# Shared expert of a mixture-of-experts layer: gate and up products from eight half-size products to seven, side by side

## The chip, the cores and the metric

The kernel runs on one core of a Trainium2 chip. The profile names the core's engines PE (TensorE, matrix products; PEld is its loading of stationary operands), DVE (VectorE), ACT (ScalarE), POOL (GpSimd) and SP (SyncE, which here only issues transfers). The metric is device time in microseconds (us) of one execution; the program is run several times and the median counts. One more execution is taken by the hardware profiler, and everything that is read engine by engine comes from that one.

## The reference

A two-layer network over a graph of 625 nodes with 1024 features each: graph attention, linear attention, a quantised feed-forward block, a graph convolution, a second linear attention, softmax attention, and last a mixture of experts. All data are 32-bit floats. The change lies in the last part:

```python
logits = xf @ Wr.T + expert_bias
rw = jax.nn.softmax(logits, axis=-1)
topw, topi = jax.lax.top_k(rw, TOP_K)
topw = jax.nn.softmax(topw, axis=-1)
combine = jnp.sum(jax.nn.one_hot(topi, NUM_EXPERTS, dtype=xf.dtype) * topw[..., None], axis=1)
shared = _swiglu(xf, sW1, sW2, sW3)
```

with `_swiglu(x, w1, w2, w3) = (silu(x @ w1.T) * (x @ w3.T)) @ w2.T`. `xf` is 625 x 1024; `sW1` (gate), `sW3` (up) and `sW2` (down) are 1024 x 1024. Each node also goes to two of eight routed experts of the same form.

## The kernel before

The node features are kept transposed, as `tT`: 128 partitions x 8 chunks of the 1024 features x 626 columns (625 nodes and one zero). Columns 0 to 312 are called `head` in the changed code, 313 to 625 `tail`. A product accumulates over feature chunks: the stationary operand is a 128 x 128 block of a weight, the moving one 313 columns of `tT`. One such matmul in the source shows as two instructions in the trace, so 256 matmuls show as x512. All are recorded at L137, in the helper `group`.

**Shared expert.** `hidden(m)`, for m = 0 to 7, makes 128 hidden features for all nodes: the gate product and the up product over all eight chunks, first for one half of the columns and then for the other, 64 instructions in all. Then ACT takes the sigmoid (L1783) and DVE multiplies twice (L1784, L1785) into `hT`. Gate and up weights come in `Half` tiles, two loads of 1 MB for 512 output columns of one matrix.

**Order.** This part stands in a `manual_schedule`: each engine's order is the order of the source. The `Stream` object `do(prep, pe, after)` writes the PE work of a step, and writes the steps that empty the accumulators (`after`) at the next call, ahead of that call's PE work. DVE, ACT and PE take their own instructions strictly in the order so written. Accumulators of the `ps2` kind are three. Weight tiles come from the pool `w`, with six buffers of 1 MB; a load waits on SP's queue until its buffer's last reader has finished, and later loads wait behind it. The pool `mid` has four larger buffers, `big` two. After the manual part the compiler's own scheduler orders the instructions.

**Routing steps.** Between the `hidden` calls stand the steps that decide who goes to which expert: `logits` (PE, 32 instructions), `turn_logits` (PE) and a chain of small DVE steps from `lg` (L1839) to `both` (L1880), here called chain one; `ranks` (PE, `prt`) and a second chain from `rank` (L1893) to `in_blk` (L1934) and `meta` (L1946), chain two; `tokens` (PE, `psl`), which gives `slots` (L1953). POOL's gathers of expert inputs (L1965) wait for `slots`, and SP reads the expert number for each weight load from `meta`. The order was: `hidden` 0, logits, `hidden` 1, turned logits, chain one, `hidden` 2, ranks, chain two, `hidden` 3, tokens, `hidden` 4 to 7.

**Experts.** `block(b)` gathers 128 rows (`xg`), transposes them on PE (`pxg`, L1972), DVE scales them into `xgT` (L1442), and then come the products with W1 and W3 (`pu`) and W2 (`pyb`), whose weights are 12 MB a block. W1 and W3 use the pool `w`, W2 the pool `mid`. The shared down projection's weights `sw2` are loaded between the blocks' weights, and `py` (last stage) uses them.

**The earlier graph layer.** One layer earlier (`Quarter`, `quarter`, `product`), the kernel already makes a block product of two halves by two halves from seven half-size products in place of eight. With blocks 11, 12, 21, 22 of the weights, DVE first makes combinations of weight tiles in place (`third`, `second`, `first`, `fourth`, all through `mix`, L1258) and of the columns (`S1` to `S4`), and adds up the seven results as they leave the accumulators (L1354). It is done twice, for two sets of columns.

Of the kernel before, what the change touches and what calls it, by code (L numbers as in the profile page):

```python
# [8 lines left out]
FP = mybir.dt.float32  # L9
# [4 lines left out]
AF = mybir.ActivationFunctionType  # L14
ALU = mybir.AluOpType
# [8 lines left out]
HN = 313  # L24
# [6 lines left out]
KC = D // 128  # L31
# [22 lines left out]
def attempt(ctx: ExitStack, tc: tile.TileContext, w: dict, out: bass.AP, shifted: bool):  # L54

    nc = tc.nc
# [10 lines left out]
    def ps2(name):  # L67
        return psums[-1][0].tile([128, 2, 512], FP, tag="ps2", name=name, bufs=3)
# [44 lines left out]
    class Half:  # L113


        def __init__(self, pool, src, c, tag="w", padded=None, now=True):
            v = src.rearrange("(k p) n -> p k n", p=128)
            self.parts = []

            def load():  # L120
                i = len(self.parts)
                t = pool.tile([128, 4, 512], FP, tag=tag, name="w", padded_shape=padded)
                self.parts.append(t)
                return nc.sync.dma_start(out=t, in_=v[:, 4 * i:4 * i + 4, c * 512:(c + 1) * 512])
# [9 lines left out]
    def group(dst, pairs):  # L134

        for i, (lhsT, rhs) in enumerate(pairs):
            made = nc.tensor.matmul(dst, lhsT=lhsT, rhs=rhs, start=(i == 0), stop=(i == len(pairs) - 1))  # L137
        latest["pe"] = made.ins.name

    latest = {}  # L140

# [13 lines left out]
    def halves(ap):  # L155
        return ap.rearrange("p (h n) -> p h n", h=2)
# [56 lines left out]
    wpool = graph.enter_context(tc.tile_pool(name="w", bufs=6))  # L213
# [3 lines left out]
    mix = mixed_up.enter_context(tc.tile_pool(name="mix", bufs=1))  # L217
# [145 lines left out]
    with ExitStack() as st0:  # L363
# [8 lines left out]
        with ExitStack() as edges:  # L372
            pool = edges.enter_context(tc.tile_pool(name="l0e", bufs=1))
# [21 lines left out]
            def load_edges():  # L395
                for dst, name in ((si, "src"), (di, "dst")):
# [16 lines left out]
                                      in_=none.unsqueeze(1).to_broadcast([128, 28, 440]))  # L413
# [4 lines left out]
            at = pool.tile([128, EN], I32, name="at")  # L418
# [24 lines left out]
            part = dict(done=0, held=0)  # L443
# [790 lines left out]
            rows_of(1, m)  # L1234
    meanT = []

    class Quarter:


        def __init__(self, i):  # L1240
            lo = 256 * i
            self.i = i
            self.tiles = {}
            self.source = {"12": ("W_self0", 512 + lo), "11": ("W_self0", lo),
                           "22": ("W_neigh0", 512 + lo), "21": ("W_neigh0", lo)}

        def room(self, name):
            self.tiles[name] = wpool.tile([128, KC, 256], FP, tag="w", name="wq" + name)

        def load(self, *names):  # L1250
            for name in names:
                self.room(name)
                src, lo = self.source[name]
                nc.sync.dma_start(out=self.tiles[name],
                                  in_=w[src].rearrange("(k p) n -> p k n", p=128)[:, :, lo:lo + 256])

        def mix(self, dst, a, b, op):
            nc.vector.tensor_tensor(self.tiles[dst], self.tiles[a], self.tiles[b], op=op)  # L1258

        def third(self):  # L1260
            self.mix("12", "22", "12", ALU.subtract)

        def second(self):
            self.mix("2", "12", "11", ALU.add)

        def first(self):
            self.mix("11", "22", "2", ALU.subtract)

        def fourth(self):
            self.mix("21", "21", "2", ALU.subtract)  # L1270

    quarters = [Quarter(0), Quarter(1)]
    quarters[0].room("2")
    quarters[0].load("12", "21", "11", "22")
    for k in range(KC):
# [55 lines left out]
    A12, A22 = ([meanT[k // 4][:, k % 4, h] for k in range(KC)] for h in (head, tail))  # L1331
    S1k, S2k, S3k, S4k = ([S[:, k, :] for k in range(KC)] for S in (S1, S2, S3, S4))

    def quarter(q):
        i = q.i
        kept = {}
        u = spool.tile([128, 2, HN], FP, tag="u", name="u", bufs=2)
        u3 = spool.tile([128, 2, HN], FP, tag="u", name="u3", bufs=2)

        def pairs(name, a, right):  # L1340
            wt = q.tiles[name]
            return [(wt[:, k, a * 128:(a + 1) * 128], right[k]) for k in range(KC)]

        def product(name, right, after):
            def pe():
                kept[0] = ps2("pw")
                for a in range(2):
                    wt = q.tiles[name]
                    group(kept[0][:, a, :HN], [(wt[:, k, a * 128:(a + 1) * 128], right[k]) for k in range(KC)])

            return lambda: do(None, pe, lambda: after(kept[0][:, :, :HN]))

        def add(dst, a, b):
            nc.vector.tensor_tensor(dst, a, b, op=ALU.add)  # L1354

        def done(c, h, a, b):
            dst = hT[c][:, 2 * i:2 * i + 2, h]
            add(dst, a, b)
            for a in range(2):
                m = 4 * c + 2 * i + a  # L1360
                nc.scalar.activation(dst[:, a, :], dst[:, a, :], AF.Relu, bias=b0_t[:, m:m + 1])

        def both(p):
            done(1, tail, p, u3)
            add(u, p, u)

# [10 lines left out]
    p1, p2, p6, p7, p4, p5, p3 = quarter(now)  # L1377
    four(sum1)
    four(sum2)
    p1()  # L1380
# [12 lines left out]
    then.third()  # L1393
    p3()
    then.room("2")
    p1, p2, p6, p7, p4, p5, p3 = quarter(then)
    p1()
    then.second()
    p2()
# [318 lines left out]

    (shifted_attention if shifted else attention)()
    wo = [Half(wpool, w["Wo"], c) for c in range(2)]  # L1720

    attn.close()
    pool = ctx.enter_context(tc.tile_pool(name="exp", bufs=1, reuse_waits="tile"))
# [37 lines left out]
        project(t)  # L1761
        turn_rows(tT, t - 1, 1)
    hT = bigT("hT")
    sw13 = [None, None]

    def hidden_halves(m):

        if m % 4 == 0:
            sw13[:] = [Half(wpool, w["sW1"], m // 4), Half(wpool, w["sW3"], m // 4)]
        w1, w3 = sw13  # L1770

        def piece(h):
            def pe():
                if h == 0:
                    hold["p13"] = [ps2("p1"), ps2("p3")]
                for p, wt in zip(hold["p13"], (w1, w3)):
                    group(p[:, h, :HN], [(wt(k, m % 4 * 128, 128), tT[:, k, h * HN:(h + 1) * HN])
                                         for k in range(KC)])

            def after():  # L1780
                p1_, p3_ = hold["p13"]
                sg = pool.tile([128, 2, HN], FP, tag="su", name="sg", bufs=2)
                nc.scalar.activation(sg, p1_[:, :, :HN], AF.Sigmoid)  # L1783
                nc.vector.tensor_tensor(sg, p1_[:, :, :HN], sg, op=ALU.mult)  # L1784
                nc.vector.tensor_tensor(halves(hT[:, m, :]), p3_[:, :, :HN], sg, op=ALU.mult)  # L1785

            do(None, pe, after if h else None)

        return piece

    def hidden(m):
        piece = hidden_halves(m)
        piece(0)
        piece(1)

    h0 = hidden_halves(0)
    h0(0)
    turn_rows(tT, NT - 1, 1)
    h0(1)
    eb_t = pool.tile([P, NE], FP, name="eb_t")  # L1800
    nc.gpsimd.dma_start(out=eb_t, in_=w["expert_bias"].to_broadcast([P, NE]))
    lg = pool.tile([P, NT, NE], FP, name="lg")
# [31 lines left out]
    nc.gpsimd.memset(place, 0)  # L1834

    do(None, logits, lambda: nc.vector.tensor_copy(halves(lgT), hold["plT"][:NE, :, :HN]))
    hidden(1)
    do(None, turn_logits)
    nc.vector.tensor_tensor(lg, hold["pl"][:P, 0:NT * NE].rearrange("p (t e) -> p t e", t=NT),  # L1839
                            eb_t.unsqueeze(1).to_broadcast([P, NT, NE]), op=ALU.add)  # L1840
# [38 lines left out]
    both = pool.tile([P, NT, NE], FP, name="both")  # L1879
    nc.vector.tensor_tensor(both, hots[0], hots[1], op=ALU.add)  # L1880
    flat = both.rearrange("p t e -> p (t e)")
    hidden(2)

    def ranks():
        hold["prt"] = ps1("prt")
# [58 lines left out]
    nc.vector.tensor_scalar(meta[:, NB + 1:NB + 2], within, -1.0, 512.0, op0=ALU.mult, op1=ALU.add)  # L1944
    nc.vector.tensor_scalar(meta[:, 0:NB], exp_f, float(NE - 1), None, op0=ALU.min)
    nc.vector.tensor_copy(meta[:, NB:NB + 1], ends[3][:, NE - 1:NE])  # L1946
    hidden(3)

    def tokens():
        hold["psl"] = ps1("psl")  # L1950
        group(hold["psl"][:, 0:NB], [(in_slot[:, i, :], in_blk[:, i, :]) for i in range(2 * NT)])

    do(None, tokens, lambda: nc.vector.tensor_scalar(slots, hold["psl"][:, 0:NB], float(N), None, op0=ALU.add))  # L1953
    for m in range(4, KC):
        hidden(m)
    do.flush()
    hand.close()

# [189 lines left out]
```

## Time and profile before

| | us |
|---|---|
| median of three runs | 2175.14 (2166.97 to 2180.34) |
| profiled execution, its own time | 2148.84 |
| its span, first to last instruction | 2147.1 |
| earlier graph layer's seven products, first to last matmul start | 777.4 to 895.3 |
| shared expert's stage, from its first matmul | 1395.4 |
| first expert's transposes (`pxg`) | 1542.4 |
| last stage (`py`) | from 2070.3 |

The profile gives each engine's busy time, and for groups of instructions the count, the busy time, the mean length of one, and the idle time of the engine just before them with what ended it. A matmul row shows the length of one instruction from start to a modelled end; neighbours overlap. Times are counted from the span's start.

### The profile page before, as it was taken

What the parts mean: (1) busy time and instruction counts of PE and PEld (TensorE: products, weight loads), DVE (VectorE), ACT (ScalarE), POOL (GpSimd) and SP (SyncE); (2) the same over time, 40 slices, a digit from 0 to 9 for tenths busy, and PEclk for the clock granted to TensorE, in tenths of its full rate; (3) what the DMA queues carried; (4) which work ended last, traced back from release to release, by engine and by line L of the source; (5) the groups of instructions that cost most, each with busy time, mean ns of one, the idle gap of its engine ahead of it and who ended that gap; (6) DMA issues with size and microseconds to landing.
All of it is one profiled execution on the core that took longest, in us unless ns stands there. A gap on an engine that the chain in (4) does not pass through costs nothing. (4 is left out here: it accounts for less than half of the span.)

```text
span 2147.1 us, 17319 instructions
## 1 busy us (share of the span) xinstructions
PE 2072.1 (97%) x6870; PEld 1184.0 (55%) x6870; DVE 754.5 (35%) x1250; ACT 197.6 (9%) x365; POOL 303.5 (14%) x321
## 2 busy tenths in 40 slices
PE   7999999399999999999999999999999999999998
PEld 6665574255446777644457776467644444444443
DVE  5786486576433772200121324222111111111012
ACT  2010110011211100000000111010000000000000
POOL 1777767200000000100000000100000000000011
PEclk9999999799999999999999999999999999999999
DMA  6632362440202102412121101202399889887832
GB/s 221 214 109 84 101 218 84 111 144 1 99 29 79 56 30 72 167 40 78 39 68 60 59 1 40 95 32 98 130 366 344 294 301 330 327 313 267 304 131 83
DMA packets 152022, 301.64 MB, mean 140 GB/s; under 512 B 12411, under 2 KB 33794, under 8 KB 151926
## 3 DMA queue, kind: packets, MB, share of 16 engines
q1 hardware_dynamic: 131356, 251.49, 33.2%
q0 software_dynamic: 15584, 38.66, 5.6%
q10 hardware_dynamic: 4986, 10.22, 1.5%
q8 instruction: 59, 0.97, 0.2%
q14 instruction: 37, 0.30, 0.0%
HBM read 277.49 MB, written 22.84 MB: 140 GB/s over the span
## 5 line engine op out<-in xcount | busy, mean ns | idle before, releaser
L137 PE MATMUL pu<-w,xgT 128*128 128x512 f32 x768 | 333.9, 593 | 1.9 <-DVE xgT L1442 1.9
L137 PEld LDWEIGHTS pu<-w,xgT 128*128 128x128 f32 x768 | 144.0, 190 | 174.8 <-issue 171.7
L137 PE MATMUL pyb<-w,hb 128*128 128x512 f32 x384 | 174.3, 599 | 2.4 <-ACT yb L105 2.1
L137 PE MATMUL pk<-w,xnT 128*125 128x512 f32 x320 | 143.5, 602 | 2.2 <-ACT xnT L1065 2.2
L137 PE MATMUL pv<-w,xnT 128*125 128x512 f32 x320 | 140.8, 593 | 0.9 <-DVE x L947 0.9
L137 PE MATMUL pq<-xnT,w 128*128 128x313 f32 x512 | 137.5, 427 | 0.8 <-DVE v L293 0.8
L137 PE MATMUL p<-tT,w 128*128 128x313 f32 x512 | 136.3, 428 | 0.4 <-DVE tT L1442 0.4
L1982 DVE TENSOR_TENSOR su<-pu,su 128x512 f32<-128x512 f32 x24 | 16.6, 691 | 314.6 <-ACT su L1981 314.6
L137 PEld LDWEIGHTS pyb<-w,hb 128*128 128x128 f32 x384 | 69.8, 189 | 90.9 <-issue 74.8
L137 PEld LDWEIGHTS pq<-xnT,w 128*128 128x128 f32 x512 | 96.9, 190 | 39.1 <-DVE v L293 1.6
L137 PEld LDWEIGHTS p<-tT,w 128*128 128x128 f32 x512 | 96.8, 190 | 37.9 <-issue 1.2
L766 PE MATMUL px<-w,oT 128*125 128x512 f32 x160 | 72.9, 615 | 32.0 <-DMA table<-es,at 26.7
L137 PEld LDWEIGHTS pk<-w,xnT 128*125 128x125 f32 x320 | 60.3, 191 | 75.8 <-issue 72.9
L137 PEld LDWEIGHTS pv<-w,xnT 128*125 128x125 f32 x320 | 59.4, 188 | 73.5 <-issue 71.2
L641 POOL DMA_INDIRECT table<-es,at x79 | 85.5, 1082 | 58.3 <-issue 28.4
L1965 POOL DMA_INDIRECT xg<-rows_d,slots x12 | 11.4, 948 | 524.7 <-PE pxg L1972 449.0
L621 POOL DMA_INDIRECT ga<-xl_d,si x79 | 79.2, 1003 | 30.1 <-issue 21.8
L621 POOL DMA_INDIRECT gb<-xr_d,di x79 | 78.6, 995 | 24.1 <-issue 20.7
L766 PEld LDWEIGHTS px<-w,oT 128*125 128x125 f32 x160 | 30.9, 196 | 71.6 <-issue 37.4
L137 PE MATMUL px<-w,hT 128*125 128x512 f32 x160 | 70.3, 592 | 0.0
L137 PE MATMUL px<-w,oT 128*125 128x512 f32 x160 | 70.3, 592 | 0.0
L137 PE MATMUL pX<-w,aT 128*125 128x512 f32 x160 | 69.3, 592 | 0.0
(376 smaller groups left out, 2443.0 us busy)
## 6 DMA issues: line engine op xcount, KB each, us to landing
w<-in_eW_dram SPq DMA_DIRECT2D x144, 1024.0 KB
w<-in_L_Wk_dram SPq DMA_DIRECT2D x8, 1024.0 KB
w<-in_L_Wv_dram SPq DMA_DIRECT2D x8, 1024.0 KB
w<-in_L_Wq_dram SPq DMA_DIRECT2D x8, 1024.0 KB
w<-in_L_Wo_dram SPq DMA_DIRECT2D x8, 1024.0 KB
w<-in_sW_dram SPq DMA_DIRECT2D x8, 1024.0 KB
table<-none SPq DMA_DIRECT2D x1, 6160.0 KB
y_d<-yb ACTq DMA_DIRECT2D x12, 512.0 KB
```

Of the source, the lines that this page charges most:

```text
L137: made = nc.tensor.matmul(dst, lhsT=lhsT, rhs=rhs, start=(i == 0), stop=(i == len(pairs) - 1))
L621: got = nc.gpsimd.indirect_dma_start(out=ab[g][side][0:p, j, :], out_offset=None, in_=src[:, :], in_offset=bass.IndirectOffsetOnAxis(ap=ix ...
L641: put = nc.gpsimd.indirect_dma_start(out=table[:, :], out_offset=bass.IndirectOffsetOnAxis(ap=at[0:p, lo + j:lo + j + 1], axis=0), in_=es[ ...
L766: made = nc.tensor.matmul(hold["px", t][:P, c, :], lhsT=oT[:, k, nodes(t)], rhs=wo[c](k), start=(k == 0), stop=(k == KC - 1 and keep is no ...
L1965: nc.gpsimd.indirect_dma_start(out=xg, out_offset=None, in_=rows_d[:, :], in_offset=bass.IndirectOffsetOnAxis(ap=slots[:, b:b + 1], axis=0))
L1982: nc.vector.tensor_tensor(su, pu[:, 0, :], su, op=ALU.mult)
```

## The change

The class `Quarter` moves to the kernel's beginning and takes the parts that its tiles are made of; for the graph layer it makes the same tiles as before. The shared expert uses it too. The blocks are the two halves of the features (`front`, chunks 0 to 3, and `back`, 4 to 7), of the output columns, and of the nodes. Each tile of 1 MB holds four chunks of the gate weight and, next to them, the same four of the up weight, for 256 output columns, so that one `mix` on DVE combines both. `eighth(i)` makes the seven products for one set of columns (i = 0, 1): each product is two halves, j = 0 for the gate and j = 1 for the up, with eight matmuls each. Results are kept in `uu` and added up as they leave the accumulators. When a gate block is complete ACT takes its sigmoid, and when the up block is complete DVE multiplies twice.

The routing steps keep their own order and now stand between single products of the first set: products one and two, logits, p6, turned logits and chain one, p7, ranks and chain two, p4, tokens, p5, p3, then the second set. `S12`, `S34` and the two `uu` take the four buffers of the pool `mid`.

```diff
-            self.source = {"12": ("W_self0", 512 + lo), "11": ("W_self0", lo),
-                           "22": ("W_neigh0", 512 + lo), "21": ("W_neigh0", lo)}
+            self.source = {name: [(src, k, lo + 512 * (name[1] == "2")) for src, k in parts[int(name[0]) - 1]]
+                           for name in ("11", "12", "21", "22")}
...
+                for src, k, lo in self.source[name]:
+                    n = k.stop - k.start
+                    nc.sync.dma_start(out=self.tiles[name][:, at:at + n, :],
+                                      in_=w[src].rearrange("(k p) n -> p k n", p=128)[:, k, lo:lo + 256])
+                    at += n
...
     wo = [Half(wpool, w["Wo"], c) for c in range(2)]
+    front, back = slice(0, 4), slice(4, KC)
+    quarters = [Quarter(256 * i, *([("sW1", k), ("sW3", k)] for k in (front, back))) for i in range(2)]
+    quarters[0].load("11", "21")
...
-    h0 = hidden_halves(0)
-    h0(0)
+    S12, S34 = (mid([128, 2, 4, HN], name) for name in ("S12", "S34"))
+    S1, S2, S3, S4 = (S[:, i] for S in (S12, S34) for i in range(2))
+
+    def eighth(i):
+        q = quarters[i]
+        uu = mid([128, 4, 2, HN], "uu")
+        kept = {}
+
+        def product(name, right, after):
+            def of(j):
+                def pe():
+                    kept[j] = ps2("ph13")
+                    for a in range(2):
+                        group(kept[j][:, a, :HN], [(q.tiles[name][:, 4 * j + k, a * 128:(a + 1) * 128], right[:, k, :])
+                                                   for k in range(4)])
+
+                do(None, pe, lambda: after(j, kept[j][:, :, :HN], uu[:, j], uu[:, 2 + j]))
...
+        def done(j, c, h, a, b):
+            dst = hT[:, 4 * c + 2 * i:4 * c + 2 * i + 2, h]
+            got = pool.tile([128, 2, HN], FP, tag="su", name="got", bufs=2)
+            if j == 0:
+                add(dst, a, b)
+                nc.scalar.activation(got, dst, AF.Sigmoid)
+                kept["gate"] = got
+            else:
+                add(got, a, b)
+                for part in (kept["gate"], got):
+                    nc.vector.tensor_tensor(dst, dst, part, op=ALU.mult)
+
+        def both(j, p, u, u3):
+            done(j, 1, tail, p, u3)
+            add(u, p, u)
+
+        return [product("11", tT[:, front, head], lambda j, p, u, u3: nc.scalar.activation(u, p, AF.Copy)),
+                product("21", tT[:, back, head], lambda j, p, u, u3: done(j, 0, head, p, u)),
+                product("2", S2, lambda j, p, u, u3: add(u, p, u)),
+                product("12", S3, lambda j, p, u, u3: add(u3, p, u)),
+                product("21", tT[:, back, tail], lambda j, p, u, u3: done(j, 0, tail, p, u3)),
+                product("11", S1, both),
+                product("22", S4, lambda j, p, u, u3: done(j, 1, head, p, u))]
+
+    now, then = quarters
+    now.load("12", "22")
+    now.room("2")
+    p1_, p2_, p6_, p7_, p4_, p5_, p3_ = eighth(0)
+    p1_()
     turn_rows(tT, NT - 1, 1)
-    h0(1)
+    add(S1, tT[:, front, tail], tT[:, back, tail])
+    nc.vector.tensor_tensor(S2, S1, tT[:, front, head], op=ALU.subtract)
+    now.third()
+    now.second()
+    then.load("12")
+    p2_()
+    now.first()
+    nc.vector.tensor_tensor(S3, tT[:, front, head], tT[:, front, tail], op=ALU.subtract)
...
-    hidden(1)
+    p6_()
+    now.fourth()
+    then.load("11")
...
-    hidden(2)
+    nc.vector.tensor_tensor(S4, tT[:, back, head], S2, op=ALU.subtract)
+    p7_()
+    then.load("22")
...
-    hidden(3)
+    p4_()
+    then.load("21")
...
-    for m in range(4, KC):
-        hidden(m)
+    p5_()
+    then.third()
+    p3_()
+    then.room("2")
+    p1_, p2_, p6_, p7_, p4_, p5_, p3_ = eighth(1)
+    p1_()
+    then.second()
+    p2_()
+    then.first()
+    p6_()
+    then.fourth()
+    p7_()
+    p4_()
+    p5_()
+    p3_()
     do.flush()
```

More of the change, by code (lines that the diff above doesn't have):

```diff
@@ L138, in group, with __init__, room, load @@
         latest["pe"] = made.ins.name
+    class Quarter:
+        def __init__(self, lo, *parts):
+            self.tiles = {}
+            self.source = {name: [(src, k, lo + 512 * (name[1] == "2")) for src, k in parts[int(name[0]) - 1]]
+                           for name in ("11", "12", "21", "22")}
+        def room(self, name):
+            self.tiles[name] = wpool.tile([128, KC, 256], FP, tag="w", name="wq" + name)
+        def load(self, *names):
+            for name in names:
+                self.room(name)
+                at = 0
+                for src, k, lo in self.source[name]:
[3 more added lines that the diff above has]
+                    at += n
+        def mix(self, dst, a, b, op):
+            nc.vector.tensor_tensor(self.tiles[dst], self.tiles[a], self.tiles[b], op=op)
+        def third(self):
+            self.mix("12", "22", "12", ALU.subtract)
+        def second(self):
+            self.mix("2", "12", "11", ALU.add)
+        def first(self):
+            self.mix("11", "22", "2", ALU.subtract)
+        def fourth(self):
+            self.mix("21", "21", "2", ALU.subtract)
+    def add(dst, a, b):
+        nc.vector.tensor_tensor(dst, a, b, op=ALU.add)
     latest = {}
@@ L1235, in attempt @@
     meanT = []
[L1237 to L1243, printed above, removed]
-            self.source = {"12": ("W_self0", 512 + lo), "11": ("W_self0", lo),
-                           "22": ("W_neigh0", 512 + lo), "21": ("W_neigh0", lo)}
[L1247 to L1272, printed above, removed]
+    every = slice(0, KC)
+    quarters = [Quarter(256 * i, [("W_self0", every)], [("W_neigh0", every)]) for i in range(2)]
     quarters[0].room("2")
@@ L1332, in attempt, with quarter @@
     S1k, S2k, S3k, S4k = ([S[:, k, :] for k in range(KC)] for S in (S1, S2, S3, S4))
-    def quarter(q):
-        i = q.i
+    def quarter(i):
+        q = quarters[i]
         kept = {}
@@ L1338, in quarter @@
         u3 = spool.tile([128, 2, HN], FP, tag="u", name="u3", bufs=2)
-        def pairs(name, a, right):
-            wt = q.tiles[name]
-            return [(wt[:, k, a * 128:(a + 1) * 128], right[k]) for k in range(KC)]
         def product(name, right, after):
@@ L1351, in product @@
             return lambda: do(None, pe, lambda: after(kept[0][:, :, :HN]))
-        def add(dst, a, b):
-            nc.vector.tensor_tensor(dst, a, b, op=ALU.add)
         def done(c, h, a, b):
@@ L1376, in attempt @@
     then.load("12")
-    p1, p2, p6, p7, p4, p5, p3 = quarter(now)
+    p1, p2, p6, p7, p4, p5, p3 = quarter(0)
     four(sum1)
@@ L1395, in attempt @@
     then.room("2")
-    p1, p2, p6, p7, p4, p5, p3 = quarter(then)
+    p1, p2, p6, p7, p4, p5, p3 = quarter(1)
     p1()
@@ L1763, in attempt @@
     hT = bigT("hT")
[L1764 to L1794, printed above, removed]
-    h0 = hidden_halves(0)
-    h0(0)
-    turn_rows(tT, NT - 1, 1)
-    h0(1)
+    S12, S34 = (mid([128, 2, 4, HN], name) for name in ("S12", "S34"))
+    S1, S2, S3, S4 = (S[:, i] for S in (S12, S34) for i in range(2))
+    def eighth(i):
+        q = quarters[i]
+        uu = mid([128, 4, 2, HN], "uu")
[8 more added lines that the diff above has]
+                do(None, pe, lambda: after(j, kept[j][:, :, :HN], uu[:, j], uu[:, 2 + j]))
+            def both():
+                of(0)
+                of(1)
+            return both
+        def done(j, c, h, a, b):
[19 more added lines that the diff above has]
+                product("22", S4, lambda j, p, u, u3: done(j, 1, head, p, u))]
```

## The prediction

> **What bounds the kernel now.** I read the page's first part, then the busy time by stretches, to see whether the shared expert's stage (1395.4 to 1542.1 us) and those around it leave TensorE idle.
>
> ```profile
> PE 2072.1 (97%) x6870; PEld 1184.0 (55%) x6870; DVE 754.5 (35%) x1250; ACT 197.6 (9%) x365; POOL 303.5 (14%) x321
> ```
> ```profile
> core 0: us, PE busy (x) PEld busy (x) DVE busy (x) ACT busy (x) POOL busy (x), PEclk, DMA share, GB/s
> 777.00:895.50 118.50, 118.50 (x452) 85.23 (x451) 42.38 (x35) 8.41 (x16) 7.67 (x13) 1.00 0.30 102
> ...
> 1395.40:1542.10 146.70, 146.26 (x575) 102.11 (x574) 28.49 (x83) 11.28 (x16) 6.32 (x11) 1.00 0.17 59
> 1542.10:2060.00 517.90, 514.23 (x1329) 233.59 (x1328) 65.16 (x96) 28.08 (x47) 9.39 (x10) 1.00 0.85 311
> ```
>
> In the changed stage PE idles 0.44 us of 146.7, at full clock, beside a DVE at 19% and DMA at 17%; the experts after it leave PE 3.7 us idle in 518. A microsecond of PE removed here comes off the end unless a new wait appears. The first stretch is the earlier graph layer, which is already made as seven products, with PE never idle. Next, the groups of the changed stage, then the rows of the earlier stage's tiles:
>
> ```profile
> L137 PE MATMUL p<-tT,w 128*128 128x313 f32 x512 | 136.3, 428 | 0.4 <-DVE tT L1442 0.4
> L137 PEld LDWEIGHTS p<-tT,w 128*128 128x128 f32 x512 | 96.8, 190 | 37.9 <-issue 1.2
> L137 PE MATMUL plgT<-tT,wr 128*8 128x313 f32 x32 | 8.6, 427 | 0.0
> ```
> ```profile
> L1354 DVE TENSOR_TENSOR hT<-pw,u x8: 809/809/810, 794.5 to 895.7; 128x626 f32<-128x626 f32 x8
> ...
> L1258 DVE TENSOR_TENSOR wq<-wq,wq x8: 2280/2282/2293, 766.7 to 854.3; 128x2048 f32<-128x2048 f32 x8
> ```
>
> A matmul is shown with 428 ns, but they overlap, so the pace counts. In the earlier stage 448 instructions of this shape run from 777.39 to 895.53, 0.2637 us each; in the changed stage 32 take 8.43 us start to start, 0.2634. Last, the timeline of the routing steps:
>
> ```profile
> 1440.33 0.19 DVE L1839 TENSOR_TENSOR lg<-plg,eb_t 125x40 f32<-125x40 f32 x1
> 1445.44 0.19 DVE L1880 TENSOR_TENSOR both<-hot,hot 125x40 f32<-125x40 f32 x1
> 1457.09 0.31 PE L137 MATMUL prt<-both,before 125*125 125x40 f32 x2
> 1458.02 0.19 DVE L1893 COPY rank<-prt 125x40 f32<-125x40 f32 x1
> 1464.73 0.34 DVE L1934 TENSOR_TENSOR in_blk<-in_blk,token 125x170 f16<-125x170 f16 x1
> 1474.60 0.41 PE L137 MATMUL psl<-in_blk,in_slot 125*128 125x17 f16 x10
> ```
>
> Chain one (lg to both) takes 5.3 us and PE asks for it 11.6 us later; chain two (rank to in_blk) takes 7.05, and PE asks 9.5 us later. That cover is what the change halves.
>
> **Removed.** Eight half-size products become seven: 512 instructions become 448 (the built order holds 224 source matmuls, two instructions each). 64 x 0.2634 = 16.9 us. A rule speaks against taking it whole: the Trainium skill, "Perfetto Trace Analysis", Identifying the Most-Contended Engine, says that the busy share of matmuls is a bad measure of how near TensorE is to its limit, and that weight loads should be read instead. Those are 102 of 146.7 us here, 70%; taken as the limit, 64 loads of 0.190 give 12.2 us. I take 16.9: the pace is a distance between starts, which no modelled end enters, and the earlier stage keeps it with the same weights and widths.
>
> Also gone: the 0.44 us in which PE waited for the last transposed rows of tT, since product two reads only the first 313 columns; and on DVE 16 instructions of 0.81 us.
>
> **Added on DVE, all beside PE if PE never waits for it.** Eight mixes of weight tiles at 2.28 = 18.2 us. S1 to S4, 1252 wide; the earlier stage does two such in 2.82, so 1.41 each, 5.6 us. Per pass (half the columns) 22 adds and multiplies 626 wide, 44 x 0.81 = 35.6 us (the multiplies lie between SBUF tiles; 0.71 by the S row, 0.81 by the hT row; I take 0.81). DVE goes from 28.5 to about 75 us in some 130: not a bound by volume. But it works in order, so each PE wait has to be followed through the first pass. With PE at 8.43 us a product:
> - PE: product one 1395.4, transposes 1.0, product two 1404.9 to 1413.4, logits to 1421.9, p6 to 1430.3, turned logits 0.7, p7 1431.0 to 1439.4, ranks 0.9, p4 1440.3 to 1448.8, token matmuls.
> - p6 needs S2 and two mixes. tT ends at 1405.8, two sums 1408.6, two mixes 1413.2; asked at 1421.9. Spare 8.7. The mixes need tiles 12 and 22, issued as their buffers come free: the four weight issues of before, which waited for the same buffers, ran from 1384.5 over 10.7 us, and the DMA they caused had ended by 1402. Spare again.
> - Ranks need chain one. Ahead of it DVE has product two's drains, two mixes, S3 and p6's drains; the last p6 drain can begin at 1430.4 and ends at 1431.2, then 5.3 us: 1436.5, asked at 1439.4. Spare 2.9. The exponential's table load is 1.3 us on ACT, which before preceded the chain, and does so again.
> - S4 and p7's drains follow (to 1440.3), then chain two from about 1440.6: in_blk at 1447.6, asked at 1448.8. Spare 1.2, the smallest.
> - Queued behind chain two is p4's first drain, 1449.3; its accumulator, one of three, is wanted by p5's second half at 1453.4. Spare 4.
>
> So I cost all DVE work at nothing, with PE as its cover. Without that cover, a late chain costs its lateness one for one. Between 0 and 3 us for the smallest spare, I take 0.
>
> **Moved loads.** The 8 MB come in 512 KB pieces with rows of 1 KB instead of 2. Between 803 and 807 a 1 MB load of such rows landed in 4.2 us at up to 378 GB/s; the longer rows reached 414. Bounds for 1 MB: 4.2, or 8.4 if the two pieces don't overlap. The latest one, tile 22 of the second pass, is issued once p7 is read (1439.5) and mixed at about 1455: hidden by either. On SP these waits stand ahead of the experts' first weights. In the built order W1 and W3 of the first block's first half are issued at about 1466, 1491, 1500 and 1508, against 1472 to about 1538 before. Then come four shared down-projection pieces (2 MB, some 5.5 us at 380 GB/s), done by 1514; the next expert weight waits for a buffer until 1516.6. W2 now waits for the sums' and u's last reader (about 1526), but stands behind W3, which waits for PE until about 1534. Cost 0; bounds minus 10 (second rival) and plus 5.5, were those pieces to hold a weight up by their whole length. POOL's gathers wait for slots, which come 24 us earlier.
>
> **Entry to the experts.** After the last product DVE has two drains before the first xgT step, and one between the two, where before it had one in all. First expert matmul after the transposes' start: 1.66 us before, now 2.4. Plus 0.7; bounds 0 and 1.5.
>
> **Sum.** -16.9 - 0.4 + 0.7 = -16.6 us. The profiled execution took 2148.84 us (span 2147.1): 2132.2, -0.77%. The median of the runs, 2175.14, is 1.2% above it; scaled alike, 2158.3, so 2158.
>
> **Rivals.** The bound is 1%, 21.7 us, about what a measurement of this kernel can tell from no change (its three runs span 13 us).
> - *Part of the gain is lost.* Weight loads set the pace (-12.2), or small waits at ranks, tokens and half-product drains take 5 to 10 us. For: the spare of 1.2, a DVE that is dense in the first pass. Against: the earlier stage has the same drains, and no PE wait. Time: 2163 to 2170.
> - *More than counted.* The experts have DMA at 0.85 in the profile; if ordinary runs, 26 us slower, are slowed there, the 2.5 MB of down-projection weights and about 1 MB of expert weights loaded earlier are worth 3.5 MB at 330 GB/s, 10 us. For: DMA at 0.9 and over in many slices. Against: PE idles there only 3.7 us. Time: 2148.
> - *Slower.* One mechanism: DVE's in-order queue takes the place of PE between product two and the tokens. Its work there is about 35 us (sums 5.6, mixes 9.1, drains 7, chains 13), as much as PE's 35. With nothing overlapped PE loses 35: 2149 - 17 + 35 = 2167, scaled 2194; with the clock falling, as to 0.7 in the one slice where PE is busy 3 tenths, some 15 more, 2209. It decides from where the waits at p6, ranks and tokens sum to over 16.6, with spares of 8.7, 2.9 and 1.2 to be used up first.
> - *It doesn't do what it says*: excluded by the built order.
>
> **How the numbers follow.** As forecast 0.72 (2158, run scatter 2150 to 2166), part lost 0.13, more 0.11, slower 0.04. Over 1% faster is below 2153.4: a fifth of the first case, most of the third, 0.24 in all. Range 2146 to 2171: it leaves out the slower case and the edges.
>
> **What would show it.** In the changed profile: x448 at 0.263 pace; the stage's first matmul to the experts' transposes 129.6 us instead of 146.9; no PE idle before S, ranks or tokens rows; mixes 2.28; ranks' matmul near 1439.5, tokens' near 1448.8; span near 2130.5. Wrong if PE rows show idle time released by DVE there, or if the saving appears and returns as PE waiting for expert weights.

## The result, and the profile after

| | before | after |
|---|---|---|
| median, 19 runs each, in us | 2176.86 (2166.97 to 2185.65) | 2156.70 (2150.10 to 2174.41) |
| profiled execution, its span | 2147.1 | 2150.7 |
| start of the shared expert's stage | 1395.44 | 1415.52 |
| stage, first matmul to the experts' transposes | 146.92 | 129.59 |
| from the transposes to the first expert matmul | 1.66 | 2.38 |
| from there to the end of the span | 603.1 | 603.2 |

The ratio over all runs, after to before, is 0.9926, with a 95% interval from 0.9911 to 0.9942, or 12.6 to 19.4 us less. The medians alone are 20.2 us apart, a little more than this interval holds; the text goes by the ratio. The forecast was 2158.0 us, a ratio of 0.9923. The profiled span did not become shorter. It must be read in two pieces: everything ahead of the stage ran 20.1 us later in this execution, and the stage with its entry into the experts gave 16.6 us back (146.92 + 1.66 before, 129.59 + 2.38 after). The work ahead of the stage has the same code in both kernels; experiments eight and nine look at it.

The first part of the page of the changed kernel, and then its busy time by stretches (start and end, length, busy time and instruction count of each engine, granted clock, share of the DMA engines, GB/s). The stretches answer those shown of before: the earlier graph layer, the shared expert's stage, the experts.

```profile
PE 2065.9 (96%) x6806; PEld 1175.4 (55%) x6806; DVE 800.0 (37%) x1290; ACT 200.4 (9%) x369; POOL 302.7 (14%) x321
```
```profile
core 0: us, PE busy (x) PEld busy (x) DVE busy (x) ACT busy (x) POOL busy (x), PEclk, DMA share, GB/s
797.60:916.00 118.40, 118.40 (x450) 84.86 (x449) 42.58 (x36) 8.41 (x16) 7.83 (x14) 1.00 0.30 103
1415.52:1545.11 129.59, 129.59 (x512) 89.89 (x510) 71.49 (x121) 14.32 (x20) 6.32 (x11) 1.00 0.30 106
1545.11:2063.60 518.49, 514.09 (x1328) 233.44 (x1327) 66.58 (x98) 28.06 (x47) 9.65 (x10) 1.00 0.83 303
```

PE is busy in all 129.59 us of the stage, so nothing that DVE does made it wait. DVE went from 28.5 to 71.5 us and is busy 55% of the time. The experts after it keep their 518 us; PE idles 4.4 us there, 0.7 more than before, and this is the entry, shown below. Next, the groups of the stage: line, engine, operation, result and operands, shapes, count, then the summed time, the mean of one in ns, and the idle time of the engine just before them.

```profile
L137 PE MATMUL ph<-S,wq 128*128 128x313 f32 x256 | 68.7, 427 | 0.0
L137 PE MATMUL ph<-tT,wq 128*128 128x313 f32 x192 | 51.5, 427 | 0.0
...
L162 DVE TENSOR_TENSOR wq<-wq,wq 128x2048 f32<-128x2048 f32 x8 | 18.3, 2283 | 0.0
L1799 DVE TENSOR_TENSOR hT<-hT,got 128x626 f32<-128x626 f32 x14 | 11.3, 807 | 1.7 <-ACT got L1794 1.4
```

256 and 192 are the 448 instructions of seven products, four from sums of columns (`S`) and three from `tT`. The multiplies at L1799 take 0.81 us, the value that was chosen. Last, PE's timeline (start, length of the run of instructions, line, operands, count, and in brackets an idle time with what ended it), and below it the DVE steps that PE asked for.

```profile
1415.52 8.60 PE L137 MATMUL ph<-tT,wq 128*128 128x313 f32 x32
...
1441.85 8.72 PE L137 MATMUL ph<-S,wq 128*128 128x313 f32 x32
...
1459.69 0.31 PE L137 MATMUL prt<-both,before 125*125 125x40 f32 x2
...
1468.78 0.40 PE L137 MATMUL psl<-in_blk,in_slot 125*128 125x17 f16 x10
...
1545.11 1.03 PE L2017 MATMUL pxg<-ident,xg 128*128 128x128 f32 x8
1547.49 16.57 PE L137 MATMUL pu<-w,xgT 128*128 128x512 f32 x38 [1.35 <-DVE xgT L1440]
```
```profile
1428.76 4.61 DVE L162 TENSOR_TENSOR wq<-wq,wq 128x2048 f32<-128x2048 f32 x2
...
1456.44 0.19 DVE L1909 TENSOR_TENSOR both<-hot,hot 125x40 f32<-125x40 f32 x1
...
1467.33 0.34 DVE L1965 TENSOR_TENSOR in_blk<-in_blk,token 125x170 f16<-125x170 f16 x1
```

No PE row of the stage carries a bracket. Three spares, the times by which a step ends before PE asks for its result, can be read off. The two mixes that p6 needs end at 1433.4, and p6 starts at 1441.85: 8.5 us. `both` ends at 1456.6 and the ranks' matmul starts at 1459.69: 3.1. `in_blk` ends at 1467.7 and the token matmuls start at 1468.78: 1.1. The wait ahead of the first expert matmul, after the stage, is 1.35 us; in the kernel before it was 0.63:

```profile
1544.02 1.55 PE L137 MATMUL pu<-w,xgT 128*128 128x512 f32 x3 [0.63 <-DVE xgT L1442]
```

### The profile page after: what moved, and what is told of

Read it like the earlier page. It is cut to its first block, busy times and chain, and to the rows that moved or that the text cites. A ratio compares the mean times of both kernels' runs of the same rounds, so it can differ in the third digit from the quotient of the medians.

```text
span 2150.7 us, 17267 instructions
## 1 busy us (share of the span) xinstructions
PE 2065.9 (96%) x6806; PEld 1175.4 (55%) x6806; DVE 800.0 (37%) x1290; ACT 200.4 (9%) x369; POOL 302.7 (14%) x321
## 5 line engine op out<-in xcount | busy, mean ns | idle before, releaser
L2027 DVE TENSOR_TENSOR su<-pu,su 128x512 f32<-128x512 f32 x24 | 16.6, 691 | 313.9 <-ACT su L2026 313.9
L137 PE MATMUL pz<-w,hT 128*125 128x512 f32 x160 | 69.0, 592 | 0.0
L137 PE MATMUL pq<-nxT,w 128*128 128x313 f32 x256 | 68.7, 426 | 0.0
L137 PE MATMUL ph<-S,wq 128*128 128x313 f32 x256 | 68.7, 427 | 0.0
```

Source lines behind the costliest of these rows:

```text
L2027: nc.vector.tensor_tensor(su, pu[:, 0, :], su, op=ALU.mult)
```

## The experiments

**One: the same surroundings, eight products.** Tiles, the loads of 512 KB, sets and the order of the routing steps stay those of the changed kernel (some loads are issued at other places), but each set is made by `straight` over all eight chunks, without mixes and sums, as four steps of 64 instructions. If the gain comes from the 64 instructions, it should vanish.

```diff
-    p1_, p2_, p6_, p7_, p4_, p5_, p3_ = eighth(0)
-    p1_()
+    def straight(i):
...
+                        group(kept[j][:, a, :HN],
+                              [(q.tiles[f"{r + 1}{c + 1}"][:, 4 * j + k, a * 128:(a + 1) * 128], tT[:, 4 * r + k, h])
+                               for r in range(2) for k in range(4)])
...
+    q1, q2, q3, q4 = straight(0)
+    q1()
...
-    add(S1, tT[:, front, tail], tT[:, back, tail])
-    now.third()
-    now.second()
...
-    p6_()
-    now.fourth()
+    q2()
...
-    p7_()
+    q3()
...
-    p4_()
+    q4()
...
```

> Keeps the tiles, the loads of 512 KB, the two sets of columns and the routing steps between them, but makes eight half-size products in place of seven (no mixes, no sums). Theory (number of matmuls at a pace of 0.2634 us): 64 instructions come back, the stage from its first matmul to the experts' transposes is 129.6 + 16.9 = 146.5 us, plus 0.4 for the wait of the logits on the last transposed rows; ratio to the kernel before 1.000 within 0.003. Rival (weight loads set the pace, so seven products were worth only 12.2 us and the rest of the gain came from layout or order): stage 142 us, ratio 0.998.

Stretches of this kernel: its stage, then the experts.

```profile
1395.95:1542.19 146.24, 146.24 (x575) 102.31 (x574) 28.36 (x83) 11.28 (x16) 6.33 (x11) 1.00 0.19 64
1542.19:2060.00 517.81, 513.86 (x1328) 233.36 (x1327) 65.17 (x96) 28.07 (x47) 9.39 (x10) 1.00 0.85 310
```

Stage 146.24 us, ratio 1.0001 (0.9990 to 1.0012). The new tiles, the smaller loads and the new places of the routing steps are worth nothing that the times show, and 0.7 us in the trace's stage (146.92 before, 0.44 of it the wait that is gone here too); the gain is in the products left out. Against the changed kernel the stage is 16.65 us longer for 64 instructions, 0.260 each, and the first expert matmul follows the transposes after 1.67 us, as before the change.

**Two: is the pace set by the columns or by the weight loads?** The second set's matmuls stream fewer columns in three of every four, in one kernel 240 (the diff) and in the other 128, with the same number of weight loads of the same size. The 73 or 185 columns left out are missing from the result.

```diff
-                        group(kept[j][:, a, :HN], [(q.tiles[name][:, 4 * j + k, a * 128:(a + 1) * 128], right[:, k, :])
-                                                   for k in range(4)])
+                        for k in range(4):
+                            n = HN if k == 0 or i == 0 else 240
+                            made = nc.tensor.matmul(kept[j][:, a, :n],
+                                                    lhsT=q.tiles[name][:, 4 * j + k, a * 128:(a + 1) * 128],
+                                                    rhs=right[:, k, 0:n], start=(k == 0), stop=(k == 3))
...
```

> In the second set of columns, three of every four accumulated matmuls stream 240 columns in place of 313 (73 columns of each are left out of the sum); their weight loads stay. 168 instructions are narrowed. Theory (the columns streamed set the pace: 0.2634 us at 313 and 0.429 at 512, so 0.83 ns a column, 0.203 at 240): stage shorter by 168 x 0.0605 = 10.2 us, 119.4 us. Rival (weight loads set it): 129.6 us, unchanged.

> The same with 128 columns (185 of 313 left out). By the columns streamed alone 0.110 us, stage 103.8 us; that is below the 0.190 us of one weight load, so here the loads should become the pace: if 0.190 us, stage 117.3 us; if loads and streams don't overlap at all, 129.6 or more.

With 240 columns the stage took 119.31 us (1427.43 to 1546.74), with 128 it took 104.05 (1416.25 to 1520.30), where the expectation was that the loads would hold it at 117.3. These two kernels and those of experiments three to five ran once each, so their stages are read and not their times. PE's timeline of the second kernel in the second set, and the busy times from its first matmul to the transposes:

```profile
1486.76 9.73 PE L1780 MATMUL ph<-tT,wq 128*128 128x313 f32 x64
1496.33 9.75 PE L1780 MATMUL ph<-S,wq 128*128 128x313 f32 x64
```
```profile
1486.76:1520.30 33.54, 33.54 (x226) 29.44 (x225) 23.51 (x25) 4.25 (x6) 0.00 (x0) 1.00 0.52 185
```

64 instructions take 9.57 us from start to start. 64 weight loads of 0.190 us one after another would take 12.2, so a load's recorded length is not what it costs. The records overlap each other too: 225 of them, some 43 us in all, lie in 33.54 us and cover 29.44. Of the 64 instructions, 16 stream 313 columns (16 x 0.2634 = 4.21 us); the other 48 share 5.36, 0.112 each, where the columns alone would give 0.110 by the expectation. So a load costs at most 0.112 us; whether it binds just below that was not tested. At 313 columns, 0.263 us, the loads are far from binding.

**Three: six of the eight mixes left out.** This takes 13.7 us of DVE work away; the products then use weights that were not mixed.

```diff
-    now.third()
...
-    now.first()
...
-    now.fourth()
...
-    then.third()
...
-    then.first()
...
-    then.fourth()
```

> Leaves out six of the eight mixes of weight tiles (13.7 us of DVE), so that the products combine the wrong blocks. Theory (DVE work is hidden): stage unchanged, 129.6 us. Rival (DVE in order is part of the bound): stage shorter.

Its stage by stretches:

```profile
1422.50:1552.10 129.60, 129.60 (x512) 89.90 (x511) 58.30 (x115) 14.33 (x20) 6.32 (x11) 1.00 0.30 106
```

DVE falls from 71.5 to 58.3 us, and the stage stays at 129.60 us. The wait ahead of the first expert matmul stays 1.35 us. Six mixes gone change nothing: they were hidden entirely.

**Four: the smallest spare used up.** `in_slot`, 1.49 us on DVE within chain two, is made four times over: 4.5 us more ahead of the token matmuls, which had 1.1 to spare.

```diff
-    nc.vector.tensor_tensor(in_slot, count_up.unsqueeze(1).to_broadcast([P, 2 * NT, 128]),
-                            at_h[:, 0, :].unsqueeze(2).to_broadcast([P, 2 * NT, 128]), op=ALU.is_equal)
+    for again in range(4):
+        nc.vector.tensor_tensor(in_slot, count_up.unsqueeze(1).to_broadcast([P, 2 * NT, 128]),
+                                at_h[:, 0, :].unsqueeze(2).to_broadcast([P, 2 * NT, 128]), op=ALU.is_equal)
```

> The changed kernel with chain two's longest step (the slot comparison, 1.41 us start to start) made four times over, with the same result. Theory: chain two is 4.2 us longer against a spare of 1.1 us, so PE idles 3.1 us before the token matmuls, stage 132.7 us. Rivals: the spare was misread and PE still doesn't wait (129.6), or the drains behind the chain hold PE as well (over 134).

PE's timeline at the token matmuls, and the stretch behind the wait:

```profile
1483.01 0.40 PE L137 MATMUL psl<-in_blk,in_slot 125*128 125x17 f16 x10 [3.36 <-DVE in_blk L1966]
1483.26 17.15 PE L137 MATMUL ph<-S,wq 128*128 128x313 f32 x64
```
```profile
1483.00:1490.00 7.00, 7.00 (x36) 5.13 (x36) 5.48 (x14) 2.72 (x3) 1.02 (x1) 1.00 0.16 53
```

Of 4.5 us added, PE waits 3.36: the spare of 1.1 absorbs the rest. The stage becomes 133.11 us, 3.52 longer. The drains queued behind chain two (the steps that empty the accumulators) start later too, but no other wait appears; p5 and p3 behind the tokens take 17.15 us as in the changed kernel, at a clock of 1.00. Here a late chain costs its lateness one for one, and no more.

**Five: the token matmuls one product earlier.** Now chain two has nothing of PE's beside it.

```diff
-    p4_()
-    then.load("21")
-
     def tokens():
...
+    p4_()
+    then.load("21")
     p5_()
```

> The changed kernel with the token matmuls set ahead of p4, so that nothing covers chain two. Theory (a late chain costs its lateness one for one): PE idles about 7.3 us before the token matmuls, stage 129.6 + 7.3 = 136.9 us. If an idle of that length also lowers the clock (the Trainium skill, TensorE: Matmul & The Clock Gate, Part 1, says that an idle window of about 3.4 us halves it): the matmuls after it run slower for a few us, stage about 139 to 140, and the granted clock of that stretch is below 1.

PE's timeline, and the stretches around the wait:

```profile
1449.19 0.43 PE L137 MATMUL psl<-in_blk,in_slot 125*128 125x17 f16 x10 [7.32 <-DVE in_blk L1965]
1449.48 10.06 PE L137 MATMUL ph<-tT,wq 128*128 128x313 f32 x32
1459.38 16.01 PE L137 MATMUL ph<-S,wq 128*128 128x313 f32 x60
```
```profile
1442.00:1449.50 7.50, 0.31 (x11) 0.31 (x11) 6.64 (x34) 0.00 (x0) 0.00 (x0) 0.73 0.42 141
1449.50:1451.00 1.50, 1.50 (x8) 1.12 (x6) 0.62 (x6) 0.00 (x0) 0.56 (x1) 0.50 0.00 0
1451.00:1453.00 2.00, 2.00 (x6) 1.29 (x6) 0.00 (x0) 0.00 (x0) 1.43 (x2) 0.67 0.38 63
1453.00:1455.00 2.00, 2.00 (x9) 1.43 (x8) 0.00 (x0) 0.00 (x0) 0.00 (x0) 1.00 0.85 299
```

The stage took 138.40 us (1396.98 to 1535.38), 8.8 more than the changed kernel: a wait of 7.32 and p4, which took 9.90 us to the next product's start instead of 8.43. The granted clock falls within the wait, is 0.50 at its end and back at 1.00 some 3 us later. The whole 7 us of chain two come back on PE as soon as no product lies beside it, and a wait of that length costs 1.5 us on top, which the 3.36 us of experiment four did not.

**Six: the entry into the experts.** The first block's gather, transposes and scaling stand ahead of the last half-size product, so that the two DVE steps on `xgT` lie beside it.

```diff
     p5_()
+    xg0 = pool.tile([128, D], FP, tag="xg", name="xg", bufs=2)
+    nc.gpsimd.indirect_dma_start(out=xg0, out_offset=None, in_=rows_d[:, :],
+                                 in_offset=bass.IndirectOffsetOnAxis(ap=slots[:, 0:1], axis=0))
+    xgT0 = pool.tile([128, KC, 128], FP, tag="xgT", name="xgT", bufs=2)
...
+    do(None, turn_first, lambda: [by_gain(xgT0[:, 4 * h:4 * h + 4, :], hold["pxg", h], 1, h, 128) for h in range(2)])
     p3_()
```

> The changed kernel with the first expert block's gather, transposes and scaling set ahead of the last half-size product. Theory: the DVE drains no longer stand between the last product and the first expert matmul; the 1.35 us wait goes, the transposes' 1.0 us stays; from the stage's first matmul to the first expert matmul 130.6 us in place of 131.97; against the kernel before 0.9920. Rival: the wait comes back at once, because the first expert matmul then waits for an accumulator that the same drains have to empty: 132 us.

PE's timeline at the entry:

```profile
1513.07 1.03 PE L2010 MATMUL pxg<-ident,xg 128*128 128x128 f32 x8
1513.94 8.62 PE L137 MATMUL ph<-S,wq 128*128 128x313 f32 x32
1522.39 16.47 PE L137 MATMUL pu<-w,xgT 128*128 128x512 f32 x38
```

The wait is gone. From the stage's first matmul (1391.92) to the first expert matmul it is 130.47 us, where the changed kernel has 131.97. Median 2128.03 us beside 2147.53 of the kernel before, ratio 0.9910 (0.9886 to 0.9934). That beats the kernel before, and in the trace this stretch is 1.5 us shorter than that of the change; whether whole runs show that much is asked below.

**Seven: the expert weights held until the stage has ended.** This asks what the earlier loads of the first block are worth, and what a late one costs.

```diff
-            w1, w3 = Half(wpool, W1, c), Half(wpool, W3, c)
+            late = not shifted and b == 0 and c == 0
+            w1, w3 = Half(wpool, W1, c, now=not late), Half(wpool, W3, c, now=not late)
+            if late:
+                for half in (w1, w1, w3, w3):
+                    half.load()
```

> The changed kernel with the first expert block's four first weight loads (4 MB) held back until the last half-size product is done. Theory (the experts are bound by PE, DMA has slack): PE waits once for the first MB to land, 4 to 5 us, then 2.7 us a MB keeps ahead of 3.45 us of matmuls; ratio to the kernel before 0.9926 + 0.002 = 0.995. Rival (in ordinary runs the experts are bound by DMA, and weights loaded ahead are worth their whole length): 4 to 5 MB at 330 GB/s, 12 to 15 us, ratio 0.998 to 1.000.

PE's timeline at the entry, and the stretches from the wait on:

```profile
1521.21 1.03 PE L2017 MATMUL pxg<-ident,xg 128*128 128x128 f32 x8
1526.62 19.34 PE L137 MATMUL pu<-w,xgT 128*128 128x512 f32 x38 [4.37 <-DMA w<-in_eW_dram]
```
```profile
1522.30:1526.60 4.30, 0.00 (x0) 0.02 (x1) 2.55 (x4) 0.00 (x0) 1.23 (x1) 0.86 0.91 311
1526.60:1532.00 5.40, 5.38 (x7) 2.30 (x8) 0.00 (x0) 0.00 (x0) 0.00 (x0) 0.50 1.03 386
1532.00:1534.00 2.00, 2.00 (x6) 0.97 (x5) 0.00 (x0) 0.00 (x0) 0.00 (x0) 0.94 1.05 392
```

The stage keeps its 129.60 us. PE then waits 4.37 us for the first weights, where the changed kernel waits 1.35 for `xgT`, so that the first expert matmul comes 135.01 us after the stage's first, 3.0 later than with the change (131.97). No later weight is waited for, but the 38 instructions behind the wait take 19.34 us where they took 16.57: the clock has fallen to 0.50 and stays there for over 5 us. That is what the longer way to the end consists of (605.9 us against 603.2). In all, holding back 4 MB costs 5.8 us, half of it by the clock. The ratio is 0.9943 (0.9925 to 0.9962), which leaves out the 0.998 and more of a DMA-bound expert stage. Against experiment six, whose entry is 1.5 us shorter, the median is 6.9 us higher (2134.97 and 2128.03, on the same chip).

**Eight and nine: the change, and the entry edit, beside each other.** The span after, which did not shrink, left two questions: whether the change itself delays the work ahead of the stage, and whether 1.5 us can be seen in whole runs. The changed kernel unaltered and the kernel of experiment six ran once more, on the same chip as experiments one, five, six and seven.

> The changed kernel unaltered. Theory (the stage gives 16.6 us whatever the work ahead of it took; the profiled execution of the changed kernel had only run that earlier work some 20 us later): from the stage's first matmul to the first expert matmul 131.9 to 132.0 us, from there to the end 603 to 604; ratio 0.9925. If the profile is on a chip where the work ahead of the stage ends near 1395, the span is near 2130.5; where it ends near 1420, near 2155. Rival (the change itself delays the work ahead of the stage by some 20 us in some executions): the stage starts near 1415 beside a kernel before whose own median stays near 2147, and the ratio then is 1.00.

> The first expert block's transposes ahead of the last half-size product, timed beside the changed kernel on the same chip. Theory (the two column steps of xgT hide behind that product): first matmul of the stage to first expert matmul 130.5 us, 1.5 us less than the changed kernel, so a ratio lower by 0.0007 (0.9918). Rival (the 1.5 us come back later as a wait for expert weights, which are issued no earlier): from the first expert matmul to the end 604.5 us or more, and the two ratios equal.

| | median | ratio | stage's start | first matmul to first expert matmul | from there to the end |
|---|---|---|---|---|---|
| kernel before | 2175.38 | | | | |
| the change | 2157.51 | 0.9924 (0.9897 to 0.9952) | 1420.57 | 131.98 | 603.15 |
| with the entry edit | 2157.42 | 0.9928 (0.9904 to 0.9953) | 1410.80 | 130.47 | 602.93 |

The same chip that had given 2147.53 for the kernel before now gave 2175.38, so the longer time is not a matter of the chip, and not of the change either: the kernel before has it too. With the entry edit the ratio was 0.9910 beside the one and 0.9928 beside the other, each within the other's interval; the change alone was timed beside 2176.86 and 2175.38 only, with 0.9926 and 0.9924.

The traces tell where the extra time arises. Shown first for experiment six (stage from 1391.92), then for the changed kernel here (stage from 1420.57): PE up to its wait for `table`, the result of the graph attention's gathers; PE's waits (engine, tile, line, what it waited for, sum, times, longest); and the group of POOL's gathers into `ga`, with POOL's idle time ahead of them.

```profile
0.00:377.83 377.83, 367.08 (x1449) 232.15 (x1449) 254.90 (x506) 47.52 (x118) 238.27 (x247) 1.00 0.46 147
```
```profile
PE px L805 <- DMA table<-es,at: 27.8, 1, 27.8
...
PE ptr L210 <- issue: 0.3, 1, 0.3
```
```profile
L660 POOL DMA_INDIRECT ga<-xl_d,si x79 | 79.8, 1010 | 30.1 <-issue 21.8 <-PE pk L137 5.6 <-PE pv L137 1.0
```
```profile
0.00:414.43 414.43, 378.34 (x1449) 234.11 (x1449) 260.17 (x516) 47.87 (x120) 245.22 (x251) 0.97 0.42 134
```
```profile
PE px L805 <- DMA table<-es,at: 20.0, 1, 20.0
...
PE pv L137 <- issue: 6.6, 6, 2.3
PE pq L137 <- DVE v L332: 6.1, 1, 6.1
PE px L805 <- issue: 4.3, 1, 4.3
PE pk L137 <- issue: 3.8, 6, 0.9
PE pct L513 <- issue: 2.5, 4, 1.1
PE ptr L210 <- issue: 1.4, 1, 1.4
```
```profile
L660 POOL DMA_INDIRECT ga<-xl_d,si x79 | 82.5, 1044 | 64.4 <-issue 23.8 <-remote 14.1 <-PE px L805 8.3
```

The same 1449 instructions take PE 36.6 us longer: 25.3 us of idle time and 11.3 us of busy time, at a mean clock of 0.97 where it had been 1.00. Of the idle time, 18.3 us are "issue", time in which PE waited for nothing that the profile shows (18.6 in the one, 0.3 in the other), in short pauses within groups of matmuls. The program orders the gathers behind PE's matmuls (`behind(got, latest["pe"])`), and POOL's idle time ahead of `ga` doubles. The wait for `table` then is 7.8 us shorter and ends at 434.44 in place of 405.67, 28.8 us later; from there to the stage's start it is 986.1 and 986.2 us. So all of the difference arises in the first 435 us, where the change does not reach. All twelve traces divide like this. Before and experiments one, five, six and seven pass the 1449 instructions in 377.6 to 378.0 us; after and experiments two, three, four, eight and nine need 403.1 to 416.1, at 0.97 or 0.98 of the clock. Kernels with the change stand on both sides. What stops PE there was not tested and stays open.

As to the entry edit: 1.5 us are in the trace and nothing of it is given back in the experts (602.93 against 603.15), so the rival falls; but the two ratios, each known to a quarter of a per cent, neither show nor exclude a gain of 0.07%.

## Why the prediction was right

**The bound.** That PE's instruction stream is the stage, and that a microsecond taken from it comes off the end, is shown by experiments one and three: 64 instructions more cost 16.65 us, and 13.7 us of DVE work less gain nothing.

**Removed, 16.9 and 0.44 us.** The stage became 17.33 us shorter against 17.3 forecast; experiment one puts 16.65 on the instructions. The price by weight loads, 12.2, is refuted for these shapes by experiment two: 64 instructions pass in 9.57 us, less than their loads' recorded lengths. It was the forecast's own step to price a removed instruction by its load; the page that it cites (the Trainium skill, "Perfetto Trace Analysis", Identifying the Most-Contended Engine) judges headroom by the loads' busy share and by the share of the peak FLOP rate. Here the loads' share, 70% before, did not show how near PE was to its limit: it idled 0.44 us of 146.7.

**Added on DVE, at nothing.** The queue was followed correctly: spares of 8.5, 3.1 and 1.1 us against 8.7, 2.9 and 1.2, the mixes 18.3 us against 18.2. DVE's busy time in the stage is 71.5 against "about 75"; three more steps of 0.8 us fall after the transposes' start. Experiment four shows that the smallest spare was real and what its loss costs.

**Moved loads, at nothing.** PE had no wait for a weight. On SP's queue the first block's four loads were issued from 1486.2, the forecast 1466 shifted by the 20.1 us of the later start. The bound of minus 10 is refuted below. That of plus 5.5 had the right size for weights that come late: holding those four back to the end of the stage cost 5.8 us. But the forecast had counted the length of the transfer alone, where half of the cost is the fallen clock behind the wait.

**Entry, plus 0.7.** 2.38 us against 2.4. Experiment six removes it.

**The rivals.** *Part of the gain is lost*: refuted in both its forms, by the pace and by a stage without idle PE. *More than counted*, 2148 us by way of DMA-bound experts: the interval of the ratio reaches to 0.9911, 2157.5 on a kernel before of 2176.9, so it is out. Its premise falls too, that ordinary runs lose their 26 us among the experts: from the first expert matmul to the end it is 603.1 us in the trace of experiment six and 603.15 in that of experiment eight, whose stage begins 28.7 us later. (The forecast's "DMA at 0.9 and over in many slices" holds for three of the page's forty.) *Slower*: its mechanism exists, as experiment five shows with 7.32 us of waiting and a halved clock, but only with the product beside chain two taken away; in the order as built none of its spares was used up.

**What failed.** One of the signs: "span near 2130.5". The forecast set its sum against one profiled execution and took for granted that another would bring the work ahead of the stage to the same moment. It came 20.1 us later, more than the gain, and the two spans put side by side would have called the change slower. The predicted time did not suffer, because it was set against the median of the runs. The factor of 1.2% between trace and median, which the forecast applied to the whole sum, need not apply to the stage: with the entry edit it took 130.47 us up to the first expert matmul, whether it began at 1391.92 or at 1410.80. On a saving of 16.6 us that is 0.2. And the 1.3 us between forecast and median are closer than these runs can tell; the interval is 6.8 us wide.

## What to carry to other kernels

Price a removed matmul by the distance between starts, and price the work that pays for it by following each in-order queue to the moment at which the bounding engine asks for the result; here both came out to a few tenths of a microsecond. Leave at least one product beside each chain of small steps, since its whole length appears on PE otherwise, and more where the clock falls with it. Compare two traces stage by stage, with the start of the stage set to zero, before reading anything from their spans.

## What the runs showed of the hardware

- A 128 x 128 weight load is recorded with 0.190 us, but matmuls that each need one followed each other at 0.112 us (128 columns): the recorded length of a load is no lower bound on the pace, and the records overlap each other (225 of them, some 43 us, within 33.54).
- After PE waits of 7.32 and 4.37 us the granted clock was 0.50, for some 3 us behind the first and over 5 behind the second, and the matmuls there lost 1.5 and 2.8 us; after one of 3.36 us it stayed at 1.00 and the products behind it kept their 17.15 us. The shorter of the two harmful waits cost more behind it, so the loss follows the time at 0.50 and not the length of the wait. The Trainium skill, "TensorE: Matmul & The Clock Gate", Part 1: The HAM clock gate, says that an idle window of some 3.4 us drops the clock to half and that a busy one as long brings it back; the two longer waits fit that, and the shorter one lies just under it. The 5 us and more at half clock are longer than one such window.
- The same kernel before, on the same chip, had medians of 2147.53 and 2175.38 us. In the traces of its variants a difference of this size lies in the first 435 us: pauses of PE of up to 2.3 us, one of 4.3, that the profile connects with nothing, a granted clock of 0.97, and gathers that follow PE. Ratios of kernels measured side by side agree.
